# A graph layer on one core: when gathered groups are summed, when fetched destinations are turned, and which engine takes one copy

## The chip, the cores and the metric

The kernel runs on one core of a Trainium2 chip. The metric is device time in microseconds (us), the median of several runs; a separate profiled execution gives the trace. The engines are TensorE (PE in the profile, its weight loads PEld), VectorE (DVE), ScalarE (ACT), GpSimd (POOL) and SyncE (SP). Each engine works through its own instructions strictly in the order in which they were written, and waits on semaphores for the others; DMA transfers are issued from SP, and gathers from POOL. PSUM is the accumulator memory that TensorE writes.

## The reference

One message-passing layer with a residual, on 6250 nodes with 64 features and 206250 edges, sorted by their destination:

```python
h = jnp.maximum(_layernorm(x, axis=-1), 0.0)
msg = h[src] + edge_attr_64
agg = jax.ops.segment_sum(msg, dst, num_segments=6250)
out = x + (jax.nn.relu(agg @ W1 + b1) @ W2 + b2)
```

## The kernel before

The sum over source nodes is made as a product of `h` with a matrix of counts: how often node s is a source of node d. Destinations are cut into windows of 3 nodes ("tiles" of edges), 6 tiles make a *step*, 14 steps a *block* of 84 tiles and 252 nodes; there are 23 blocks (numbers 0 to 22). The program is written as one loop over steps n, with block b = n // 14 and s = n % 14 the step in its block, and what stands at a step goes out on all engines at once:

* every third step VectorE makes one-hot codes for 18 tiles (`hotb`, L975; its inputs `at`, `of` come from `encode`, L958 and L964);
* at every odd step TensorE counts 12 tiles into PSUM (`count`, `pc`, L991; two such buffers), and ScalarE copies them as floats into `ring` (L1004);
* at s = 1, 5 and 7 TensorE multiplies 16, 16 and 17 slices of `h` with the block before (`products`, `pv`, L1013), and at s = 8 VectorE adds the result into the sums (L1045, L1047);
* the edge features are loaded in chunks (`feat`, L491), and at s = 9, 11, 13 summed by destination with a one-hot `hotf` (L504) into a PSUM bank (`chunk_sum`, L515). At s = 0 of the next block `take_sums` (L523) copies the bank to `by_node`, and at s = 3 `chunk_place` (L545) puts it into `pv`. For block 0 the copy is at step 19 and the placing at step 20.

To know where a chunk's edges go, their destinations are needed. They come in five *lots* t = 0 to 4: POOL gathers a lot (`fetch_dst`, the tile `dstq`, 1.5 KB in each of 128 rows), VectorE turns it into numbers within the chunk (`chunk_nodes`, L455 and L456, which wait for the gather's landing), TensorE transposes it (`chunk_turn`, `pdst`, L463), and ScalarE stores it as `rel` (L464). `hotf` of a later block, and some checks at s = 8, read `rel`. The transposes write a PSUM tile with the tag `po`, of which there is one buffer. The same buffer serves, in turn, the two products of the output layer (`mlp_hidden`, `ph`, L1090, read by ScalarE's relu L1092; `mlp_product`, `po`, L1100, read by VectorE L1117) and the value turns of the source lists (`pw`, L796, read by ScalarE L817). Whoever writes it next waits until the last reader is done. The output layer for finished nodes runs at s = 11 (`ph`), 13 (`po`) and 14, from block 9 on.

The last 20 of 202 edge groups (1024 edges each; 182 to 201) take another way: POOL gathers the rows of `h` (`hrows`, L361), VectorE adds them to the edge features (`add_rows`, L1180, at a step that a planner sets from its own estimates of when they have landed), then makes a one-hot (`group_hot`, L566), and two steps later TensorE sums the group (`sum_group`, L576, 8 products), ScalarE copies the result (L578), and three steps after that VectorE adds it into the sums at an address that it reads at run time (`add_sums`, L558). Once a group is summed, its buffer `pfeat` (two of them) is loaded again (L1133), and after `add_rows` the gathers of the next group but one are queued on POOL. At which s a group may be made hot stands in `GROUPS` (1 and 3; in the last block 1 and 5), at most one at each, if a group with its rows added is there. POOL's gathers go out in runs of three, each released by a tiny copy (L1164) that waits for VectorE or for `by_node`.

## Time and profile before

| | us |
|---|---|
| median of 3 runs (377.62, 378.62, 378.67) | 378.62 |
| the profiled execution | 378.36 |
| its span, first to last instruction | 376.7 |
| TensorE busy in it | 333.4 |
| ScalarE, VectorE, POOL busy | 319.4, 318.2, 243.7 |

The span leaves 1.7 us of the profiled execution's time outside. "Busy" of a matmul is modelled, so an engine shown as 100% busy in a stretch is one that was not seen to wait. In the rows of the timeline the columns are: start in us from the span's start, duration in us, engine, line and operation, output and inputs, how many instructions were merged into the row, and in brackets how long the engine sat idle before it and what ended that idle time.

### The profile page before, as it was taken

The page shows a single profiled execution, that of the slowest core. Times are in us where ns is not written, and L with a number is a line of the kernel's source. Part 1 is how long each engine was busy: PE and PEld are TensorE (multiplying, and loading weights), DVE is VectorE, ACT ScalarE, POOL GpSimd, SP SyncE. Part 2 cuts the span into 40 slices and gives each one's busy share as a digit, 9 for nine tenths or more (in the row PEclk, how much of TensorE's full clock was granted, in tenths as well). Part 3 has the DMA queues.
Part 4 walks back from the last instruction along what each step waited for, and adds up shares of the span by engine and source line. Part 5 has one row for each costly group of instructions (what it writes and reads, how often), then busy time and mean ns, then how long its engine had stood idle before and what let it go on. Part 6 is the DMA issues. An engine that isn't in the chain of part 4 may idle for free.

```text
span 376.7 us, 17450 instructions
## 1 busy us (share of the span) xinstructions
PE 333.4 (89%) x7311; PEld 304.7 (81%) x7312; DVE 318.2 (84%) x863; ACT 319.4 (85%) x365; POOL 243.7 (65%) x300
## 2 busy tenths in 40 slices
PE   2055888999989998979999999999999999999993
PEld 1035777988978988968989899989989989998882
DVE  5879998999988999978897998979997898988510
ACT  6678988999789799977999899998999889998820
POOL 8475058888888677675777588887887677721000
PEclk9999999999999999998999999999999999999997
DMA  7855979586685797693876976956967966974400
GB/s 160 269 183 149 339 238 325 153 249 194 199 251 164 211 274 203 172 294 90 264 216 181 288 203 190 293 166 205 303 178 202 307 182 169 278 220 144 124 6 18
DMA packets 97237, 77.75 MB, mean 206 GB/s; under 512 B 14279, under 2 KB 90175, under 8 KB 97152
## 3 DMA queue, kind: packets, MB, share of 16 engines
q1 hardware_dynamic: 88370, 66.72, 58.2%
q0 software_dynamic: 6544, 9.06, 9.9%
q8 instruction: 59, 0.97, 1.1%
q10 hardware_dynamic: 2238, 0.79, 0.9%
q14 instruction: 26, 0.21, 0.2%
HBM read 72.28 MB, written 4.26 MB: 203 GB/s over the span
## 4 chain that ended last, share of the span: by engine, by line
PE 65%; DVE 9%; DMA 7%; ACT 4%; issue 3%; SPq 2%; POOL 1%; DVEq 0%; ACTq 0%; POOLq 0%
PE pv L1013 29%; PE pc L991 11%; PE bank L515 10%; PE ph L1090 4%; PE po L1100 4%; DVE hotb L975 3%; ACT ring L1004 3%; PE bank L576 2%; PE pv L545 2%; DMA feat<-in_edge 2%; DMA dstq<-in_dst_g,cols_i 2%; DMA pfeat<-in_edge 1%; PE pk L789 1%; DVE hotf L504 1%; DMA hrows<-table,src_p 1%
## 5 line engine op out<-in xcount | busy, mean ns | idle before, releaser
L1004 ACT ACTIVATE ring<-pc 128x1764 fp32r<-128x1764 uint8 (+2 forms) x180 | 257.5, 1485 | 24.9 <-PE pc L991 21.0
L361 POOL DMA_INDIRECT hrows<-table,src_p x156 | 170.2, 1091 | 43.9 <-issue 40.6
L1013 PE MATMUL pv<-ring,h 128*128 128x252 f32 (+1 forms) x1127 | 148.6, 285 | 0.4
L1013 PEld LDWEIGHTS pv<-ring,h 128*128 128x128 f32 x1127 | 136.4, 190 | 1.4 <-ACT ring L1004 0.5
L975 DVE TENSOR_TENSOR hotb<-at,of 127x576 int32<-127x576 bf16 x212 | 118.3, 601 | 1.3 <-issue 0.3
L991 PE MATMUL pc<-hotb 128*128 128x49 fp8e5 x1904 | 77.4, 186 | 7.0 <-ACT ring L1004 3.5
L991 PEld LDWEIGHTS <-hotb 128*128 128x128 fp8e5 x1904 | 66.0, 98 | 20.2 <-issue 10.3
L515 PE MATMUL bank<-feat,hotf 128*18 128x64 f32 x3240 | 59.2, 220 | 4.9 <-DVE hotf L504 3.5
L515 PEld LDWEIGHTS bank<-feat,hotf 128*18 128x18 f32 x3240 | 47.1, 98 | 8.5 <-DVE hotf L504 4.3
L504 DVE TENSOR_TENSOR hotf<-rel,iota 128x432 f32<-128x432 bf16 (+1 forms) x68 | 40.7, 600 | 0.1
L1164 POOL COPY root<-root 1x1 f32<-1x1 f32 x43 | 17.3, 403 | 34.7 <-DVE root L1174 34.5
L361 POOL DMA_INDIRECT sums<-in_dst_g,sums x15 | 14.6, 970 | 15.7 <-ACT sums L379 12.0
L958 DVE TENSOR_TENSOR at<-iota_a,kq 128x576 bf16<-128x576 bf16 (+1 forms) x53 | 23.9, 450 | 0.3
L361 POOL DMA_INDIRECT words<-packed,first_i x15 | 17.5, 1167 | 8.4 <-DVE firstp L709 4.2
L1047 DVE TENSOR_TENSOR sums<-sums,pv 128x144 f32<-128x144 f32 (+3 forms) x24 | 7.1, 323 | 18.6 <-PE pv L1013 18.4
L809 ACT ACTIVATE kq<-pk 128x512 bf16<-128x512 f32 (+17 forms) x48 | 17.7, 454 | 3.6 <-PE pk L789 3.6
L964 DVE TENSOR_TENSOR of<-of,kv 128x288 bf16<-128x288 bf16 (+1 forms) x53 | 16.7, 316 | 2.8 <-DVE of L958 0.5
L1092 ACT ACTIVATE after<-ph,b1s 128x504 f32<-128x504 f32 (+4 forms) x16 | 9.4, 589 | 8.1 <-PE ph L1090 8.1
L958 DVE TENSOR_TENSOR of<-iota_w,kq 128x288 bf16<-128x288 bf16 (+1 forms) x53 | 16.0, 301 | 0.0
L523 DVE COPY after<-bank 128x384 f32<-128x384 f32 (+2 forms) x23 | 12.5, 545 | 3.4 <-PE bank L515 3.0
L576 PE MATMUL bank<-after,pfeat 128*64 128x42 f32 x312 | 13.6, 233 | 1.9 <-DVE after L566 1.9
L1090 PE MATMUL ph<-sums,w1s 128*128 128x504 f32 (+4 forms) x32 | 14.7, 542 | 0.4 <-DVE sums L1047 0.4
(203 smaller groups left out, 337.6 us busy)
## 6 DMA issues: line engine op xcount, KB each, us to landing
feat<-in_edge SPq DMA_DIRECT2D x135, 384.0 KB
pfeat<-in_edge SPq DMA_DIRECT2D x19, 256.0 KB
hrows<-table,src_p POOLq DMA_INDIRECT x156
out_y<-after SPq DMA_DIRECT2D x9, 126.0 KB
xl<-in_x SPq DMA_DIRECT2D x2, 512.0 KB
table<-xl SPq DMA_DIRECT2D x2, 512.0 KB
after<-in_x SPq DMA_DIRECT2D x4, 252.0 KB
table<-xl SPq DMA_DIRECT2D x1, 544.0 KB
```

What stands on the lines that cost most here:

```text
L361: nc.gpsimd.indirect_dma_start(out=rows, out_offset=None, in_=source, in_offset=bass.IndirectOffsetOnAxis(ap=index, axis=0), compute_op=op)
L504: nc.vector.tensor_tensor(hot_of[u][:, :n].rearrange("p c j w -> p (c j) w"), rel[:, c:c + n].rearrange("p c q k -> p (c q k)").unsqueeze( ...
L515: nc.tensor.matmul(bank[q * QP:q * QP + WQ, at:at + D], hot_of[u][:, c, j, :], feats[u][c][:, j, :], start=(k == 0), stop=(k == JP - 1))
L576: nc.tensor.matmul(pa[k:k + D, :], tiles[:, j, :], hot[:, j, :], start=(j < 2), stop=(j >= n - 2))
L809: nc.scalar.activation(kq[:, q, at:at + n].rearrange("s i k o -> s (i k) o"), pk[:, q, a:a + n].rearrange("s i k -> s (i k)").unsqueeze(2) ...
L958: nc.vector.tensor_tensor(to[:, :n].rearrange("s i k (m o) -> s (i k) m o", o=2), iota_k.rearrange("s (m o) -> s m o", o=2).unsqueeze(1).t ...
L975: nc.vector.tensor_tensor(hot[:SLOTS, :n, c:c + m * A8].rearrange("s i (w a) -> s i w a", a=A8), at[:SLOTS, o:o + n, k].unsqueeze(2).to_br ...
L991: nc.tensor.matmul(pc[:, at:at + HI], hot[:, :P], hot[:, P:P + HI], start=True, stop=True)
L1004: nc.scalar.activation(to[:, h0:h1], of[:, h0:h1, u:v, :V], AF.Copy)
L1013: nc.tensor.matmul(pvs[b], h2[k][:, h - thirds[k][0], :], ring[:, h, c:c + columns_of_block(b)], start=(h == 0), stop=(h == HI - 1))
L1090: nc.tensor.matmul(ph, w1s, agg[:, a:z], start=True, stop=True)
L1164: nc.gpsimd.tensor_copy(root[0:1], sign)
```

## The change

```diff
-GROUPS = (1, 3)
-LAST_GROUPS = (1, 5)
+GROUPS = {1: 2}
+LATE_GROUPS = {1: 1, 3: 1}
+LAST_GROUPS = {1: 1, 5: 1}
...
     def take_sums(b):
         n = sum(units[u][2] for u in of_block[b]) * D
         by_node[b] = spare["by_node"]
-        nc.vector.tensor_copy(by_node[b][:, :n], bank[:, :n])
+        if b:
+            nc.vector.tensor_copy(by_node[b][:, :n], bank[:, :n])
+        else:
+            nc.scalar.activation(by_node[b][:, :n], bank[:, :n], AF.Copy)
...
     for t in range(1, NT):
         n = 78 + 14 * t
         before.setdefault(n, []).append(lambda t=t: t > 1 and at_once(GATHER_US, lambda: fetch_dst(t)))
-        n = 48 if t == 1 else 87 + 14 * t
+        n = 71 if t == 1 else 93 + 14 * t
         before.setdefault(n, []).append(lambda t=t: chunk_nodes(t))
         before.setdefault(n + 2 + (t > 1), []).append(lambda t=t: chunk_turn(t))
...
-            if s in (GROUPS if b < NW - 1 else LAST_GROUPS) and h_next < added:
+            of = GROUPS if b < NW - 3 else LATE_GROUPS if b < NW - 1 else LAST_GROUPS
+            for _ in range(min(added - h_next, of.get(s, 0))):
                 group_hot(h_next)
                 at_step(n + 2, features_h, h_next)
                 h_next += 1
```

Up to block 19 groups are made hot only at s = 1, up to two of them, and so summed at s = 3 and added at s = 6; before, also one at s = 3, summed at 5 and added at 8. Blocks 20 to 22 stay as they were. The groups that move: 183 waits from block 4 (s = 3) for block 5 and goes with 184; 185 goes from block 6 to block 7, with 186; 188 from block 9 (hot at step 129, summed at 131) to block 10 (141, 143); 189, 190 and 191 each go from s = 3 of blocks 10, 11, 12 to s = 1 of blocks 11, 12, 13; 192 and 193 are summed together in block 14, 194 and 195 in block 16. The others, and from 196 on all, keep their steps. The steps of `add_rows` and POOL's whole order stay. Since a buffer is loaded again when its group is summed, those loads move with the groups.

Lot 1 of the destinations is worked on at step 71 (before 48) and turned at 73 (before 50), both in block 5. Lots 2, 3 and 4 go from steps 115, 129, 143 to 121, 135, 149, and their turns from 118, 132, 146 to 124, 138, 152: from s = 3 and 6 to s = 9 and 12. The gathers that fetch them keep their steps (106, 120, 134). Lot 0 is as before. The copy of block 0's bank goes from VectorE to ScalarE.

Three places in the order that the program writes out. The line numbers in these rows are those of each kernel: the changed one's are higher by 1 up to `chunk_sum` and by 4 below `take_sums` (its L979 is L975 before, its L1008 is L1004, its L464 and L465 are L463 and L464).

The first is VectorE from step 128 to step 131, in block 9. `dstq` is lot 3, the L1180 and L566 are group 188's. Before:

```order
L964 TENSOR_TENSOR of<-of,kv 128x288
L455 TENSOR_SCALAR dstq<-dstq,cols 128x384
L456 SCALAR_TENSOR_TENSOR dstq<-iota_q,cols,dstq 128x384
L975 TENSOR_TENSOR hotb<-at,of 127x18x32
L975 TENSOR_TENSOR hotb<-at,of 127x18x16
L504 TENSOR_TENSOR hotf<-rel,iota 128x432
L1180 TENSOR_TENSOR pfeat<-pfeat,hrows 128x512
L566 TENSOR_TENSOR after<-dst_p,iota 128x336
L755 TENSOR_SCALAR near<-words,nfirst 128x128 x2
```

and with the change:

```order
L968 TENSOR_TENSOR of<-of,kv 128x288
L979 TENSOR_TENSOR hotb<-at,of 127x18x32
L979 TENSOR_TENSOR hotb<-at,of 127x18x16
L505 TENSOR_TENSOR hotf<-rel,iota 128x432
L1184 TENSOR_TENSOR pfeat<-pfeat,hrows 128x512
L759 TENSOR_SCALAR near<-words,nfirst 128x128 x2
```

The two `dstq` instructions and the group's one-hot have left; the addition of the gathered rows has stayed.

The second is TensorE at steps 137 and 138, in the same block, where the first output layer meets the turn of lot 3. Before:

```order
L991 LDWEIGHTS hotb
L991 MATMUL pc<-hotb 128x49
L515 MATMUL bank<-feat,hotf 18x64 x24
L1090 MATMUL ph<-sums,w1s 128x504
L991 LDWEIGHTS hotb
```

and with the change:

```order
L995 LDWEIGHTS hotb
L995 MATMUL pc<-hotb 128x49
L516 MATMUL bank<-feat,hotf 18x64 x24
L1094 MATMUL ph<-sums,w1s 128x504
L464 MATMUL pdst<-shift,dstq 128x128 x3
L995 LDWEIGHTS hotb
```

The three transposes now stand between the layer's first product and the next count; it is the same at steps 151 and 152 with lot 4. Before, they stood six steps earlier, behind `pv` and a group's sum.

The third is ScalarE in block 5, steps 71 to 75, with the turn of lot 1. Before:

```order
L1004 ACTIVATE ring<-pc 128x49x36
L817 ACTIVATE kv<-pw 128x248
L817 ACTIVATE kv<-pw 128x264
L1004 ACTIVATE ring<-pc 128x49x36
L578 ACTIVATE after<-bank 128x42
```

and with the change:

```order
L1008 ACTIVATE ring<-pc 128x49x36
L821 ACTIVATE kv<-pw 128x248
L821 ACTIVATE kv<-pw 128x264
L465 ACTIVATE rel<-pdst 128x384
L1008 ACTIVATE ring<-pc 128x49x36
L582 ACTIVATE after<-bank 128x42 x2
```

The store of `rel` stands behind the two copies of the value turn, whose PSUM buffer the transposes take over, and two groups' results are copied instead of one. On TensorE the transposes stand right behind `pw` there.

## The prediction

> **What bounds the kernel now.** I read the chain of waits first, then the engines' busy time in stretches of 10 us, then the timeline wherever TensorE shows idle time.

> ```profile
> PE 333.4 (89%) x7311; PEld 304.7 (81%) x7312; DVE 318.2 (84%) x863; ACT 319.4 (85%) x365; POOL 243.7 (65%) x300
> PE 65%; DVE 9%; DMA 7%; ACT 4%; issue 3%; SPq 2%; POOL 1%; DVEq 0%; ACTq 0%; POOLq 0%
> 100.00:110.00 10.00, 8.38 (x290) 7.86 (x287) 9.37 (x29) 7.63 (x9) 8.46 (x10) 1.00 0.85 249
> 160.00:170.00 10.00, 7.28 (x149) 6.52 (x146) 7.94 (x22) 7.43 (x6) 7.05 (x9) 1.00 0.92 279
> 170.00:180.00 10.00, 10.00 (x236) 8.86 (x231) 8.35 (x26) 7.74 (x10) 5.69 (x7) 0.83 0.44 121
> 190.00:200.00 10.00, 10.00 (x265) 8.88 (x262) 9.21 (x24) 9.65 (x12) 7.33 (x9) 1.00 0.85 246
> ```

> In the stretches the columns are PE, PEld, DVE, ACT, POOL, granted clock, DMA share, GB/s. TensorE carries the chain. From 170 us on it is seen to wait almost nowhere, so there only its own work and new waits count. Before that it idles in a few places, most of all in 160 to 170, behind which the clock falls to 0.83.

> **What the change removes: the wait in block 9.** The next rows are POOL's gather of lot 3, VectorE, and TensorE.

> ```profile
> 159.46 0.95 POOL L361 DMA_INDIRECT dstq<-in_dst_g,cols_i  x1 [0.30 <-DVE of L958]
> 165.84 2.12 PE L1013 MATMUL pv<-ring,h 128*128 128x252 f32 x16
> 166.04 0.42 DVE L455 TENSOR_SCALAR dstq<-dstq,cols 128x384 f32<-128x384 int32 x1 [1.92 <-DMA dstq<-in_dst_g,cols_i]
> 166.49 0.62 DVE L456 SCALAR_TENSOR_TENSOR dstq<-iota_q,cols,dstq 128x384 f32<-128x384 int16 x1
> 168.58 0.69 DVE L1180 TENSOR_TENSOR pfeat<-pfeat,hrows 128x512 f32<-128x512 f32 x1
> 169.18 0.51 DVE L566 TENSOR_TENSOR after<-dst_p,iota 128x336 f32<-128x336 f32 x1
> 169.74 0.67 PE L576 MATMUL bank<-after,pfeat 128*64 128x42 f32 x16 [1.79 <-DVE after L566]
> 174.70 0.47 PE L991 MATMUL pc<-hotb 128*128 128x49 fp8e5 x12
> 172.00:173.00 1.00, 1.00 (x6) 1.00 (x6) 1.00 (x2) 1.00 (x1) 0.52 (x2) 0.50 0.54 203
> ```

> The lot lands 6.6 us after its issue; VectorE stands still for 1.92 us, everything behind is late, and group 188's one-hot, made two steps before its sum, comes 1.79 us after TensorE wants it. About 1.1 us later the clock is halved for some 3 us (0.17 of 10 us missing, at half rate: 3.4). With the change both `dstq` instructions move behind the next six steps, and the group's one-hot and sum into block 10. `hotb` then starts at about 164.1, and nothing on TensorE waits for L1180. What this gives: `pv` ends at 165.84 + 2.12 = 167.96, and the count after the next `pv` starts at 174.70, 6.74 us on. The same pieces where nothing waits:

> ```profile
> 186.44 0.67 PE L576 MATMUL bank<-after,pfeat 128*64 128x42 f32 x16
> 187.04 0.61 PE L463 MATMUL pdst<-shift,dstq 128*128 128x128 f32 x3
> 187.49 0.46 PE L991 MATMUL pc<-hotb 128*128 128x49 fp8e5 x12
> 189.85 0.47 PE L991 MATMUL pc<-hotb 128*128 128x49 fp8e5 x12
> ```

> Count and `pv` take 189.85 - 187.49 = 2.36. Of the rest, 4.38, a group's sum (187.04 - 186.44 = 0.60) and the transposes (187.49 - 187.04 = 0.45) are only moved: **3.33 us gained**, 1.79 of it the wait and most of the other 1.5 the half clock. The bounds: 1.9 if the clock falls all the same, 3.33 if not. I take 3.33, since the half clock directly follows the longest wait of the second half.

> **What it adds: three waits for the one `po` buffer.** At step 138 the transposes of lot 3 follow `ph` and must wait until ScalarE's relu has read it; at 152 lot 4 does the same.

> ```profile
> 177.09 1.11 PE L1090 MATMUL ph<-sums,w1s 128*128 128x504 f32 x2
> 178.04 0.46 PE L991 MATMUL pc<-hotb 128*128 128x49 fp8e5 x12
> 175.20 3.17 ACT L1004 ACTIVATE ring<-pc 128x1764 fp32r<-128x1764 uint8 x2 [1.33 <-PE pc L991]
> 178.26 0.68 ACT L1092 ACTIVATE after<-ph,b1s 128x504 f32<-128x504 f32 x1
> 193.20 0.46 PE L991 MATMUL pc<-hotb 128*128 128x49 fp8e5 x12
> 193.42 0.69 ACT L1092 ACTIVATE after<-ph,b1s 128x504 f32<-128x504 f32 x1
> ```

> The relu ends at 178.94; with 0.06 for the semaphore (178.26 against the product's end at 178.20) the transposes start at 179.00, where the count started at 178.04: **0.96 lost**, and by 193.42 + 0.69 + 0.06 - 193.20 **0.97** in block 10. Queued behind the wait are the count, whose ring copy ScalarE waits for, and all later TensorE work, which is the bound here, so nothing absorbs it. Below this it cannot go, as the relu must run; upwards each grows by up to a ring copy (3.17 / 2 = 1.59) if ScalarE is behind. I take the lower end, as ScalarE has lost `rel`'s copy from the steps before. `mlp_product` two steps later finds `rel` stored (0.49, row below) before it.

> In block 5 the transposes of lot 1 follow `pw` and wait for ScalarE's two `kv` copies.

> ```profile
> 105.50 0.28 PE L991 MATMUL pc<-hotb 128*128 128x49 fp8e5 x3
> 106.05 1.22 ACT L809 ACTIVATE kq<-pk 128x248 bf16<-128x248 f32 x4
> 107.40 0.40 PE L991 MATMUL pc<-hotb 128*128 128x49 fp8e5 x9 [1.62 <-issue]
> 107.83 1.65 ACT L1004 ACTIVATE ring<-pc 128x1764 fp32r<-128x1764 uint8 x1 [0.56 <-PE pc L991]
> 109.76 0.50 PE L991 MATMUL pc<-hotb 128*128 128x49 fp8e5 x12
> 110.00 0.66 ACT L817 ACTIVATE kv<-pw 128x248 bf16<-128x248 f32 x2 [0.52 <-PE pw L796]
> 164.79 0.32 PE L991 MATMUL pc<-hotb 128*128 128x49 fp8e5 x6 [0.80 <-DVE of L964]
> 0.00:105.90 105.90, 75.58 (x1622) 67.84 (x1623) 95.23 (x253) 88.66 (x113) 70.97 (x106) 1.00 0.76 225
> 0.00:164.30 164.30, 130.41 (x2896) 118.78 (x2897) 149.27 (x412) 141.96 (x173) 115.75 (x155) 1.00 0.76 222
> q8 instruction: 59, 0.97, 1.1%
> ```

> As it stands the wait is 110.66 + 0.06 - 109.76 = 0.96. But just ahead TensorE idles 1.62 us in the middle of a count, with no releaser. It does so once more at 164, and 5793 - 3245 = 2548 multiplications and loads lie between: close to ten times 256, and 59 packets of instructions for 14623 of them are 248 each. I read it as waiting for instructions, at a fixed place in the stream. By then the changed TensorE has issued 38 fewer (group 183's sum 32, the transposes 6), so the place moves behind into `pv` (18 of the count, 20 of the 32 in `pv`, about 1.7 us of work), while its fetch starts only about 0.5 us later: 1.62 shrinks to about 0.4. Then ScalarE sets the pace: kq ends 107.27, ring copy 108.92, `kv` 109.58 or a little more with `pw` late; transposes at 109.7, count at 110.2, against 109.76 + 0.45 moved work. **Block 5: 0**, bounds -0.6 and +0.96; I take 0.

> [...]

> **What costs nothing.** The copy on ScalarE and the two one-hots together:

> ```profile
> 52.75 1.65 ACT L1004 ACTIVATE ring<-pc 128x1764 fp32r<-128x1764 uint8 x1 [0.51 <-PE pc L991]
> 54.58 0.55 PE L545 MATMUL pv<-select,after 128*64 128x42 f32 x12
> 62.48 0.67 PE L515 MATMUL bank<-feat,hotf 128*18 128x64 f32 x24 [0.63 <-DMA feat<-in_edge]
> 187.69 0.49 ACT L464 ACTIVATE rel<-pdst 128x384 bf16<-128x384 f32 x1 [0.33 <-PE pdst L463]
> L566 DVE TENSOR_TENSOR after<-dst_p,iota 128x336 f32<-128x336 f32 (+1 forms) x20 | 9.9, 493 | 0.0
> ```

> ScalarE gets to the copy behind the ring copy, at 54.40, and needs some 0.49 for its 384 columns, so TensorE's placing waits 0.4. Eight us later it waits 0.63 for edge features, whose loads were issued before: covered, else +0.4. POOL's first gathers leave 0.7 later; the first `add_rows` they feed has behind it 2 us of VectorE time, as lot 1 has left. In block 5 VectorE takes 1.04 (lot 1) and 0.49 more ahead of a `hotb` that TensorE needs some 3 us later: free. Lot 2, behind step 120's sums, delays one `hotb` by **0.1**; bound 1.04. TensorE's and ScalarE's numbers of instructions are the same but for that copy, and a moved sum still costs 0.60.

> Sum: -3.33 + 0.96 + 0.97 + 0 + 0.1 = **-1.3 us**. Against the execution's own 378.36 that is 377.1, against the median of the runs, 0.26 higher, 377.3; I say **377.2**.

> **The rivals.**
> * *A, the new waits fall into slack* (375.3): TensorE's 100% hides time in which VectorE or ScalarE set the pace, and the 1.93 us of blocks 9 and 10 cost nothing. For it: ScalarE is at 9.65 of 10 in 190 to 200. Against: the ring copies there wait for TensorE (1.33 above).
> * *B, the half clock stays* (378.6): the stage at 171 comes from something other than the wait, and 1.45 less is gained. For it: the idle of 1.62 at 105.8 drew no such stage. Against: it begins a us behind 1.79 of idle that follows 0.80.
> * *C, slower* (380.4): ScalarE comes to the relu a ring copy late, as the counts reach it closer together; each of the two waits then holds 1.59 more. It decides once ScalarE's copy of the previous count ends after `ph`; at 178.2 both end within 0.2 us of each other. Against: ScalarE has 0.49 less to do just before.
> * *D, block 5 pays* (378.2): the idle at 105.8 stays, or moves on to another place, and the `kv` wait counts in full, +0.96.

> [...]

> **How the numbers follow.** Forecast 0.45 (376.4 to 378.0), A 0.14, B 0.15, C 0.12, D 0.14. A difference under 0.3%, 1.1 us, can't be told from none. Faster: 0.30 of the forecast, A, and 0.04 of B and D, 0.48. Same: 0.15 of the forecast, 0.20 of B and D, 0.35. Slower: C and 0.05 of B and D, 0.17. The range takes in A, and B and D with 0.7 above, and leaves out C: 375.2 to 379.3.

> **What would show it.** Right: L455 no longer waits for a DMA; no idle at L576 in block 9, and a clock of 1.00 in 165 to 180; before the transposes of lots 3 and 4 an idle of 0.9 to 1.0 released by L1092; the 1.62 before L1013's products in block 5 down to under 0.7. Wrong: a clock stage of 0.5 somewhere after all, waits for L1092 of over 2 us, or TensorE waiting for a `hotb` in blocks 5 to 8 for longer than before.

## The result, and the profile after

| | us |
|---|---|
| before, median of 6 executions (377.62 to 381.13) | 378.64 |
| the change, median of 6 (381.06 to 385.61) | 383.73 |
| ratio, with its 95% interval | 1.0128 (1.0087 to 1.0169) |
| the change's profiled execution, and its span | 381.06, 379.3 |

The change made the kernel slower by 1.3%, where 0.4% faster was forecast. The profiled execution is the fastest of the six: its mean granted clock is 0.995, that of the others 0.980 to 0.993, so the trace shows less than the median lost.

The view of TensorE's waits, by what it waited for (total us, times, longest). First the change, then, in a fence of its own, the kernel before:

```profile
PE bank L580 <- ACT after L582: 5.1, 4, 2.0
PE pdst L464 <- ACT after L1096: 1.6, 2, 0.8
PE pdst L464 <- ACT kv L821: 0.8, 1, 0.8
PE pc L995 <- DVE hotb L979: 0.6, 2, 0.4
PE pxn L895 <- issue: 0.6, 1, 0.6
PE bank L516 <- issue: 0.5, 1, 0.5
PE pv L1017 <- issue: 0.2, 1, 0.2
```

```profile
PE bank L576 <- DVE after L566: 1.9, 2, 1.8
PE pc L991 <- issue: 1.6, 1, 1.6
PE pc L991 <- DVE hotb L975: 0.9, 1, 0.9
PE pc L991 <- DVE of L964: 0.8, 1, 0.8
```

The second and third rows of the change are the waits for the `po` buffer that the prediction named. The first is one that it did not: four times TensorE waited 1 to 2 us before a group's sum, for ScalarE's copy (L582) of another group. With the half clock, these rows add up to nearly the difference of the two profiled executions, 381.06 - 378.36 = 2.70: new are 5.1 + 1.6 + 0.8; gone are 1.8 for the one-hot of group 188, 0.3 at the one-hots `hotb`, 1.1 at the pauses that no data ends (1.6 + 0.8 before, the 0.8 listed as L964 among them; 0.6 + 0.5 + 0.2 now), and 1.7 for the half clock (a stage of 3.4 us at half rate, which the trace before has and the trace of the change has not). That makes 7.5 - 4.9 = 2.6; the changes in the rows not shown cancel.

The wait in the timeline of the change, at the pair of block 7 (two sums at one step):

```profile
137.98 0.92 DVE L570 TENSOR_TENSOR after<-dst_p,iota 128x336 f32<-128x336 f32 x2
138.53 0.67 PE L580 MATMUL bank<-after,pfeat 128*64 128x42 f32 x16
138.75 0.75 ACT L821 ACTIVATE kv<-pw 128x408 bf16<-128x408 f32 x2
139.28 1.76 ACT L1008 ACTIVATE ring<-pc 128x1764 fp32r<-128x1764 uint8 x1
140.80 0.34 ACT L582 ACTIVATE after<-bank 128x42 f32<-128x42 f32 x1
141.19 0.67 PE L580 MATMUL bank<-after,pfeat 128*64 128x42 f32 x16 [1.98 <-ACT after L582]
```

The first group's sum ends at 139.20. Its copy stands on ScalarE behind the `kv` copies and a ring copy, runs from 140.80 to 141.14, and only then does the second sum start. The two groups use different columns of one PSUM tile, `bank` (`b = g % 2` in `sum_group`), and both one-hots were ready: what orders them is that the program writes sum, copy, sum, copy, and the second sum, a write to the tile, starts 0.05 us behind the end of the copy, the last read of it. Before, two groups were never summed at one step, and the copy was long done. The other pairs, in blocks 5, 14 and 16, waited 0.96, 0.99 and 1.18.

### The profile page after: what moved, and what is told of

The parts are those of the page before. It is cut to its first block, busy times and chain, and to the rows that moved or that the text cites. A ratio compares the mean times of both kernels' runs of the same rounds, so it can differ in the third digit from the quotient of the medians.

```text
span 379.3 us, 17435 instructions
## 1 busy us (share of the span) xinstructions
PE 332.4 (88%) x7311; PEld 303.2 (80%) x7312; DVE 317.4 (84%) x862; ACT 319.8 (84%) x366; POOL 245.5 (65%) x300
## 4 chain that ended last, share of the span: by engine, by line
PE 48%; ACT 5%; DVE 2%; issue 2%; POOL 2%; DMA 1%; DVEq 0%; ACTq 0%; POOLq 0%
PE pv L1017 21%; PE bank L516 8%; PE pc L995 8%; PE po L1104 4%; ACT ring L1008 3%; PE ph L1094 3%; PE bank L580 2%; PE pv L549 2%; DMA hrows<-table,src_p 1%; PE pk L793 1%; POOL hrows L362 1%; ACT kq L813 1%; DVE hotb L979 1%; POOL words L362 1%; ACT after L1096 1%
## 5 line engine op out<-in xcount | busy, mean ns | idle before, releaser
L1008 ACT ACTIVATE ring<-pc 128x1764 fp32r<-128x1764 uint8 (+2 forms) x180 | 258.1, 1484 | 26.4 <-PE pc L995 23.2
L979 DVE TENSOR_TENSOR hotb<-at,of 127x576 int32<-127x576 bf16 x212 | 118.2, 601 | 1.0
L995 PEld LDWEIGHTS <-hotb 128*128 128x128 fp8e5 x1904 | 65.2, 98 | 15.9 <-issue 7.5
L516 PE MATMUL bank<-feat,hotf 128*18 128x64 f32 x3240 | 60.2, 220 | 5.5 <-DVE hotf L505 3.2
L580 PEld LDWEIGHTS bank<-after,pfeat 128*64 128x64 f32 x312 | 11.7, 138 | 5.9 <-ACT after L582 5.6
L1096 ACT ACTIVATE after<-ph,b1s 128x504 f32<-128x504 f32 (+4 forms) x16 | 9.4, 589 | 8.1 <-PE ph L1094 8.1
L1168 POOL COPY root<-after 1x1 f32<-1x1 f32 x22 | 7.7, 352 | 12.8 <-DVE after L525 9.6
```

The costliest lines, as they stand in the source:

```text
L516: nc.tensor.matmul(bank[q * QP:q * QP + WQ, at:at + D], hot_of[u][:, c, j, :], feats[u][c][:, j, :], start=(k == 0), stop=(k == JP - 1))
L580: nc.tensor.matmul(pa[k:k + D, :], tiles[:, j, :], hot[:, j, :], start=(j < 2), stop=(j >= n - 2))
L979: nc.vector.tensor_tensor(hot[:SLOTS, :n, c:c + m * A8].rearrange("s i (w a) -> s i w a", a=A8), at[:SLOTS, o:o + n, k].unsqueeze(2).to_br ...
L995: nc.tensor.matmul(pc[:, at:at + HI], hot[:, :P], hot[:, P:P + HI], start=True, stop=True)
L1008: nc.scalar.activation(to[:, h0:h1], of[:, h0:h1, u:v, :V], AF.Copy)
L1168: nc.gpsimd.tensor_copy(root[0:1], sign)
```

## The experiments

**Both sums, then both copies.** The order on every engine stays that of the change, instruction for instruction; only what the second sum waits for differs.

```diff
+    def features_of(gs):
+        copies = []
+        for g in gs:
+            read_bases(g, 1)
+            copies.append(sum_group(g, parts_of.pop(g), copied=False))
+        for g, copy in zip(gs, copies):
+            copy()
+            if g + ROWS < G:
+                load_h(g + ROWS)
...
-                at_step(n + 2, features_h, h_next)
+                at_step(n + 2, features_of, gs)
```

> The change with one thing reordered: where two groups are summed at one step, both sums are written before ScalarE's two copies, so that the second sum no longer has to wait for the copy of the first out of the shared PSUM tile. Every engine has the same instructions in the same order as in the change. Theory P (the pair's wait is what the change lost): the four waits of 0.96, 1.98, 0.99 and 1.18 us before a second sum are gone, the profiled execution comes to about 376 (381.06 less 5.1), the median to 376 to 378.5, and the mean granted clock is no lower than before's. Rival R (the new waits for the po buffer and the later one-hots set the time): the median stays at 382 or more. Rival K (the clock falls in the changed kernel for another cause than those waits): the waits go, but the median stays 2 us or more above the profiled execution, at 379 to 381, with mean clocks of about 0.98.

Measured: 376.01 (375.18 to 377.96), ratio to the kernel before 0.9941 (0.9913 to 0.9969). The pair of block 7 in its timeline:

```profile
139.03 1.13 PE L580 MATMUL bank<-after,pfeat 128*64 128x42 f32 x32
139.26 0.75 ACT L825 ACTIVATE kv<-pw 128x408 bf16<-128x408 f32 x2
139.79 1.76 ACT L1012 ACTIVATE ring<-pc 128x1764 fp32r<-128x1764 uint8 x1
140.10 0.47 PE L999 MATMUL pc<-hotb 128*128 128x49 fp8e5 x12
141.31 0.44 ACT L583 ACTIVATE after<-bank 128x42 f32<-128x42 f32 x2
```

The 32 products run in 1.13, the copies are as late as before, and nobody waits for them. The change as it stands is 7.7 us slower than this kernel (383.73 - 376.01, beside 378.64 and 378.85 for the kernel before). 5.1 of it are the waits; the other 2.6 go along with the clock, of which the median over the executions is 0.994 here and 0.9845 in the change, but that the waits lower the clock is argued, not shown, by this run. Theory P holds in the median, and R falls. P's number for the profiled execution, about 376, was missed: it is 377.96, the slowest of the eight, with a half-clock stage at 63 us. K falls for the most part: the clock comes back with the waits gone.

**The groups at their old steps**, with the rest of the change:

```diff
-GROUPS = {1: 2}
+GROUPS = {1: 1, 3: 1}
```

> The change with the groups at their old steps (one at s = 1, one at s = 3); the later destinations and the copy on ScalarE stay. Theory P: no pair is left, and the sum of the prediction holds for the rest: 376.4 to 378.0, with 0.8 us of wait each before the transposes of lots 3 and 4. Rival R: 381 or more, since the waits for the po buffer are all still there.

Measured: 379.23 (377.19 to 382.19), ratio 1.0009 (0.9978 to 1.0040). No pair, no loss; but the 1.3 us of the prediction's sum aren't there either. TensorE's waits in its trace:

```profile
PE pc L995 <- issue: 1.5, 1, 1.5
PE pc L995 <- DVE hotb L979: 1.4, 3, 0.9
PE pdst L464 <- ACT after L1096: 0.8, 1, 0.8
PE pdst L464 <- DVE root L1178: 0.8, 1, 0.8
PE pdst L464 <- ACT kv L821: 0.7, 1, 0.7
```

The wait of 1.8 in block 9 is gone, but the pause of 1.5 in block 5 has stayed, and the three waits of the transposes stand beside it. That is as the prediction's rival D has it; but here group 183's sum, whose move was to shorten the pause, stays where it was, so the run is no full test of D.

**The groups alone** at their new steps; destinations and copy as before, sum and copy of a pair in turn.

> Of the change only the groups' new steps; destinations and the copy as before. Theory P: four waits before a second sum, 5 us in all, against some 1.8 to 3.3 us gained in block 9, since group 188 no longer stands behind the late lot: 380 to 383. Rival R: 378.6 or less, as no transposes stand behind the relu.

Measured: 383.89 (380.31 to 385.33), ratio 1.0124 (1.0078 to 1.0170): the whole loss of the change, without the destinations, and 0.9 more than theory P's 383. Four waits for ScalarE's copy, 5.6 us. Here the half clock also follows a wait before a second sum, of 2.00 us, from 140.39 to 142.39; busy time and granted clock in stretches of 1 us (columns as above):

```profile
140.00:141.00 1.00, 0.39 (x14) 0.27 (x10) 1.00 (x5) 1.00 (x4) 0.69 (x2) 1.00 0.95 281
141.00:142.00 1.00, 0.00 (x0) 0.00 (x0) 1.00 (x3) 1.00 (x1) 0.83 (x1) 1.00 1.10 345
142.00:143.00 1.00, 0.61 (x12) 0.61 (x14) 1.00 (x5) 0.34 (x2) 0.86 (x1) 0.65 1.01 331
143.00:144.00 1.00, 1.00 (x23) 0.92 (x20) 0.90 (x4) 0.21 (x1) 0.81 (x3) 0.50 0.98 323
144.00:145.00 1.00, 1.00 (x8) 1.00 (x6) 0.90 (x4) 0.87 (x1) 0.69 (x2) 0.50 0.79 171
145.00:146.00 1.00, 1.00 (x8) 1.00 (x8) 1.00 (x3) 0.78 (x1) 0.70 (x1) 0.65 0.64 238
```

**The turns ahead of the layer's first product**, pairs as in the change:

```diff
-        n = 71 if t == 1 else 93 + 14 * t
+        n = 71 if t == 1 else 92 + 14 * t
...
-        before.setdefault(n + 2 + (t > 1), []).append(lambda t=t: chunk_turn(t))
+        before.setdefault(n + 2, []).append(lambda t=t: chunk_turn(t))
```

> The change with lots 2 to 4 worked on one step sooner (s = 8) and turned two steps sooner (s = 10), ahead of the layer's first product instead of behind it; the pairs stay. Theory P: the two waits of 0.8 us for the relu go, 1.6 us in all, and the pairs' 5.1 us stay: profiled execution about 379.5, median 381 to 383. Rival R: 378 or less, as the waits for the relu are gone.

Measured: 382.92 (381.91 to 385.92), ratio 1.0133 (1.0096 to 1.0171). The two waits for the relu are gone from the trace, 0.6 for lot 3's own numbers has come, and the time isn't told apart from the change's. The waits for the relu were not what made it slow. P's median holds; its number for the profiled execution, about 379.5, was missed (382.85).

**Pairs alone, without the wait**, destinations and copy as before:

> The kernel of the pairs alone, both sums ahead of the copies, once more: its first run fell on a chip on which the kernel before took 474 us with TensorE pausing all over the program, so nothing could be told there. Theory P (the waits are all that the pairs cost): 5 us under the same kernel with the copies between (383.9), so 377 to 379. Theory L (the later destinations carry the gain of the kernel with everything, 376.0): no less than 378, with VectorE still waiting about 1.9 us for lot 3 in block 9 and TensorE about 1.5 for the one-hots behind it. Rival G (pairing carries the gain, since group 188 leaves block 9 and TensorE's pause without a releaser in block 5 gets shorter): 376 to 377.

Measured: 374.79 (371.94 to 379.82), ratio 0.9906 (0.9867 to 0.9944). Against the groups alone with sum and copy in turn (1.0124) the order of two calls in the program is worth 2.2%, with the same instructions on every engine. Its timeline in block 9, where the prediction wanted the destinations out of the way:

```profile
162.29 0.42 DVE L456 TENSOR_SCALAR dstq<-dstq,cols 128x384 f32<-128x384 int32 x1 [0.40 <-DMA dstq<-in_dst_g,cols_i]
164.84 0.68 DVE L1185 TENSOR_TENSOR pfeat<-pfeat,hrows 128x512 f32<-128x512 f32 x1
165.09 2.22 PE L1018 MATMUL pv<-ring,h 128*128 128x252 f32 x17
168.68 0.31 PE L996 MATMUL pc<-hotb 128*128 128x49 fp8e5 x6 [1.21 <-DVE hotb L980]
```

Lot 3 is still worked on there, and VectorE waits 0.40 for it. With group 188 gone from the block, TensorE goes on to the next `pv` and waits 1.21 for a one-hot, where it waited 1.79. This is a lucky trace, the fastest of the twelve executions: the lot landed 5.0 us after its issue, and 6.6 in the kernel before. In the trace of the groups alone, with the lots at the same steps, it landed 6.3 us after its issue, and the waits are larger:

```profile
170.68 0.47 DVE L456 TENSOR_SCALAR dstq<-dstq,cols 128x384 f32<-128x384 int32 x1 [1.62 <-DMA dstq<-in_dst_g,cols_i]
177.12 0.31 PE L992 MATMUL pc<-hotb 128*128 128x49 fp8e5 x6 [1.53 <-DVE hotb L976]
```

G holds for the median, and goes further than it said; but the groups' move alone does not take the wait behind the late lot away, as theory L had it for this block.

**The change without the wait, and one part taken back at a time**: the turns of lots 2 to 4 ahead of the product, as in the diff above; then lot 1 at steps 48 and 50 (`48 if t == 1`); then block 0's copy on VectorE.

> The change with both sums of a pair ahead of their copies and the turns of lots 2 to 4 ahead of the layer's first product, once more. If the waits of 0.8 us for the relu lie on the path: 376.0 less 1.6, plus up to 0.65 for VectorE's work on lot 3: 374.4 to 375.3. If they fall into slack: 376.0.

Measured: 378.11 (375.21 to 380.81), ratio 0.9999 (0.9960 to 1.0038).

> The change with both sums of a pair ahead of their copies and lot 1 back at steps 48 and 50, once more. If the wait of 0.75 us for the kv copies in block 5 lies on the path: 375.3; if VectorE's 1.04 us in block 3 is paid for: 376 to 377.

Measured: 374.25 (373.51 to 375.79), ratio 0.9913 (0.9876 to 0.9949).

> The change with both sums of a pair ahead of their copies and block 0's copy back on VectorE, once more. If the copy costs and gains nothing: 376.0 within 0.5; if ScalarE's lateness in block 1 is paid for: 375.7; if VectorE's relief there is worth its 0.5 us: 376.5.

Measured: 377.38 (374.49 to 378.96), ratio 0.9967 (0.9929 to 1.0005).

The first came out slower than both of its expectations. Its two waits for the relu are gone, but its executions spread over 5.6 us, and its profiled one, 380.77, has 2.4 us of pauses that no data ends ahead of 66 us and three half-clock stages (its mean clock is 0.981); of TensorE's waits there:

```profile
PE bank L516 <- issue: 2.5, 3, 1.7
PE pc L999 <- DVE hotb L983: 1.3, 1, 1.3
PE pdst L464 <- ACT kv L825: 0.7, 1, 0.7
PE pxn L899 <- issue: 0.7, 1, 0.7
```

So this run doesn't settle what the turns' place is worth. Between the marks of blocks 10 and 11 in the table below it gains 0.31 on the kernel before where the kernels with late turns lose 1.2; there the wait is on the path. Lot 1's move looks like the part whose return gives most: 374.25, below both of its expectations, is 1.8 below the first kernel of this section and 3.1 below the one with the copy on VectorE, which both have lot 1 late. As ratios, 0.9913 against 0.9941 and 0.9967, the intervals overlap. In the table below, the stretch from block 3 to 5 is 2.1 us shorter with lot 1 early than in the first kernel: 0.45 are the transposes, which then stand ahead of block 3's mark, 0.75 is the wait, and two pauses that no data ends, 0.67 and 0.47, are in the first kernel's trace alone. The kernel with the copy on VectorE came out above all three of its expectations. The copy's own share isn't told apart: 0.9967 with it on VectorE against 0.9941 on ScalarE, and the intervals overlap.

Where in the program each kernel stands against the one before, from the starts of VectorE's addition of `pv` at s = 8 in the profiled executions (minus is ahead, us). "No wait" is the first experiment, "pairs alone" and "lot 1 early" are those without the wait too:

| block | before, start | change | no wait | pairs alone | lot 1 early | turn early |
|---|---|---|---|---|---|---|
| 1 | 57.63 | 0.05 | 0.10 | -0.92 | 0.10 | 0.62 |
| 3 | 85.72 | 0.33 | 1.44 | -0.92 | 1.60 | 4.13 |
| 5 | 115.95 | 1.79 | 2.14 | -2.08 | 0.18 | 5.67 |
| 8 | 158.10 | 1.30 | 1.15 | -2.20 | -0.77 | 6.06 |
| 9 | 174.89 | -1.30 | -1.69 | -4.85 | -3.62 | 3.40 |
| 10 | 190.04 | -1.80 | -2.27 | -6.20 | -4.20 | 2.09 |
| 11 | 204.65 | -0.62 | -1.09 | -6.71 | -3.02 | 1.78 |
| 16 | 275.38 | 2.73 | -0.60 | -6.20 | -2.51 | 2.56 |

The rows behind two of its entries, of the kernel before and of the change:

```profile
158.10 0.47 DVE L1047 TENSOR_TENSOR sums<-sums,pv 128x144 f32<-128x144 f32 x2
174.89 0.42 DVE L1047 TENSOR_TENSOR sums<-sums,pv 128x252 f32<-128x252 f32 x1 [0.31 <-PE pv L1013]
```

```profile
159.40 0.48 DVE L1051 TENSOR_TENSOR sums<-sums,pv 128x144 f32<-128x144 f32 x2
173.59 0.40 DVE L1051 TENSOR_TENSOR sums<-sums,pv 128x252 f32<-128x252 f32 x1
```

Behind block 16 the distances stay within 0.4 us. From block 1 to 3 they move by up to 3.5 us between kernels that differ in nothing that matters there: in these blocks TensorE waits for edge features, in another way each time (1.3 us in the kernel before, 1.5 in the change, 2.3 without the wait and with the copy on VectorE), and half-clock stages fall there, as the one at 63 us in the first experiment.

**Runs in another condition.** Ten runs met a condition of the chip in which the kernel before takes 474 to 489 us, so that they can't be compared with the others. Four are the kernels from "pairs alone" to the copy on VectorE, a first time (e5 to e8):

> Of the change only the groups' new steps, with both sums of a pair written before the two copies; destinations and block 0's copy as before. The pairs' waits are gone here. Theory P (those waits are all that the pairs cost): 5 us under the same kernel with the copies between (383.9), so 377 to 379. Theory L (the later destinations carry the gain of the kernel with everything, 376.0): no less than 378, with VectorE still waiting about 1.9 us for lot 3 in block 9 and TensorE about 1.5 for the one-hots behind it. Rival G (pairing carries the gain, since group 188 leaves block 9 and TensorE's pause without a releaser in block 5 gets shorter): 376 to 377.

> The change with both sums of a pair ahead of their copies, and lots 2 to 4 worked on at s = 8 and turned at s = 10, ahead of the layer's first product. If the waits of 0.8 us for the relu lie on the path: 376.0 less 1.6, plus up to 0.65 for VectorE's work on lot 3, which the transposes then wait for: 374.4 to 375.3. If they fall into slack: 376.0.

> The change with both sums of a pair ahead of their copies, and lot 1 back at steps 48 and 50. If the wait of 0.75 us for the kv copies in block 5 lies on the path: 376.0 less 0.75, so 375.3; VectorE's 1.04 us for the lot, back in block 3, is paid for if TensorE's waits for one-hots there grow: then 376 to 377.

> The change with both sums of a pair ahead of their copies, and block 0's copy back on VectorE. The prediction's reading is that the copy costs and gains nothing: 376.0 within 0.5. If ScalarE's lateness in block 1 is paid for (the placing waits 0.25 us for it): 375.7; if VectorE's relief there is worth its 0.5 us: 376.5.

Measured, as ratios to the kernel before there: 0.9984 (0.9926 to 1.0042), 1.0148 (1.0083 to 1.0213), 1.0110 (1.0047 to 1.0172) and 1.0229 (1.0169 to 1.0289). In this condition three of the four are slower than the kernel before, so what the other runs say of them is not shown for every chip.

The others were to settle what moving lots 2 to 4 gives: lot 1 early and the turns ahead of the product (e13), the same with the copy on VectorE (e14), and all destinations at their old steps (e16), each without the wait of the pairs; then repetitions of the first and the last.

> Both sums of a pair ahead of their copies, lot 1 at its old steps, lots 2 to 4 worked on at s = 8 and turned at s = 10, ahead of the layer's first product; the copy of block 0 on ScalarE. If the move gains in block 9 and gives it back behind the relu (0.8 us in block 9, 0.8 in block 10), this kernel keeps it: 1.0 to 1.6 under the same with turns behind the product (374.25, 0.9913 of before), so 372.7 to 373.3, or 0.987 of before. If the move has nothing to gain once the group has left block 9: 374.3, 0.991.

> The kernel before this one in the list (both sums first, lot 1 at its old steps, lots 2 to 4 turned at s = 10) with block 0's copy back on VectorE. If the copy's engine costs and gains nothing: the same within 0.5 us. If the 1.4 us by which the other pair of kernels differed (377.38 against 376.01, on two chips) belongs to the copy: 1.4 slower.

> Both sums of a pair ahead of their copies, block 0's copy on ScalarE, and every lot of destinations at its old steps. If moving lots 2 to 4 gains by itself: slower than 374.25 (0.9913 of before) by 1 us or more, with VectorE waiting 1.9 us for lot 3 and TensorE 1.2 for the one-hots behind it. If the groups' move carried the gain of block 9: 374.3 or less, 0.991 or less.

Measured: 1.0023 (0.9941 to 1.0105), 0.9993 (0.9933 to 1.0053) and 1.0078 (1.0009 to 1.0147).

> Once more: both sums of a pair ahead of their copies, lot 1 at its old steps, lots 2 to 4 worked on at s = 8 and turned at s = 10, ahead of the layer's first product; the copy of block 0 on ScalarE. If the move gains in block 9 and gives it back behind the relu (0.8 us in block 9, 0.8 in block 10), this kernel keeps it: 1.0 to 1.6 under the same with turns behind the product (374.25, 0.9913 of before), so 372.7 to 373.3, or 0.987 of before. If the move has nothing to gain once the group has left block 9: 374.3, 0.991.

> Both sums of a pair ahead of their copies, lot 1 at its old steps, lots 2 to 4 worked on at s = 8 and turned at s = 10, ahead of the layer's first product; the copy of block 0 on ScalarE. If the move gains in block 9 and gives it back behind the relu (0.8 us in block 9, 0.8 in block 10), this kernel keeps it: 372.7 to 373.3, or 0.987 of before. If the move has nothing to gain once the group has left block 9: 374.3, 0.991.

> Both sums of a pair ahead of their copies, block 0's copy on ScalarE, and every lot of destinations at its old steps. If moving lots 2 to 4 gains by itself: slower than 374.25 (0.9913 of before) by 1 us or more. If the groups' move carried the gain of block 9: 374.3 or less, 0.991 or less.

Measured: 1.0060 (0.9983 to 1.0137), 1.0037 (0.9989 to 1.0085) and 1.0065 (0.9979 to 1.0151). Whether a kernel with lot 1 early, the turns ahead of the product and no wait beats 374.3 stays open.

## Why the prediction was wrong, step by step

* **The step that failed** is in "What costs nothing": TensorE's number of instructions is the same, "and a moved sum still costs 0.60". The second sum of a pair costs 0.60 and a wait for ScalarE's copy, 0.96, 1.98, 0.99 and 1.18 us: 5.1, against a sum of -1.3. With both sums ahead of the copies the same kernel gains, so these waits are what turned the forecast gain into a loss. The prediction followed the three waits for one PSUM buffer, `po`, and did not ask the same of the other buffer that the change makes two writers meet in, `bank`. In all four pairs the second sum waited for the copy, though it writes other columns; whether only the order that the program sets for any two users of one tile holds it back, no run here shows. With sums before copies the rest of the change comes to 0.9941, 2.2 us under the kernel before where 1.3 was forecast.
* **Block 9, -3.33**: from block 8's mark to block 10's the kernel before takes 31.94, the change 28.84. Of those 3.10 us, 0.60 (one group's sum) has only moved on behind block 10's mark, and 0.80 of new wait is in it: 3.10 - 0.60 + 0.80 = 3.3 removed; 3.6 without the pairs' waits. (The transposes cancel: lot 4's have left the stretch, and lot 2's have come in, as the rows below show.) The size was right. How much of it each move gives is less clear: with the lots moved and the group left, the same reckoning gives 3.1, and the 1.8 of wait is gone; with the group moved and the lots left, it gives 3.4 in the lucky trace of the pairs alone and 2.1 in that of the groups alone, and 1.2 to 1.5 of wait stays. So the two moves overlap for the most part: credited one by one they would count more than 3.6, and the lots' move pays 1.6 behind the relu. In the medians it shows no gain on top of the groups' (0.9913 with it, lot 1 early and the copy on ScalarE; 0.9906 without).
* **The waits behind the relu, 0.96 and 0.97**: 0.80 each, as the prediction's mechanism has it.
* **Block 5, 0**: `kv` is waited for 0.76, and the pause has moved into `pv`, behind its 11th product, and shrunk from 1.62 to 0.20, much as written (20 of its 32 instructions would be the 10th, and 0.4 was named). From block 3's mark to block 5's the change takes 1.46 more, 0.96 of it the pair and 0.45 lot 1's transposes, which stood just ahead of block 3's mark before: about 0 for the rest, as written. What this 0 hides is that the groups' move alone makes the stretch 1.2 us shorter in its trace (pairs alone in the table: -0.92 to -2.08), a gain that the kernels with lot 1 late do not show.
* **The copy on ScalarE**: the placing waits 0.3 for it, 0.4 was named; its price can't be told from nothing.
* **The rivals.** B, the half clock stays, is wrong of the place: the profiled execution has no such stage between 165 and 180. It may be right of the kernel: the other five executions have clocks of 0.980 to 0.993, so that stages are likely in them, but no trace shows where. C gave the right sign, which was luck: its 380.4 is about a third of the loss, and its mechanism isn't there, as no wait for L1096 is longer than 0.8. The signs named for being right were nearly all seen (the line that was L455 no longer waits for a DMA, no idle before a group's sum in block 9, full clock from 165 to 180, 1.62 down to 0.20; the idle behind the relu was 0.80 instead of 0.9 to 1.0), and the kernel was slower all the same: none of the rivals, and nothing in "what would show it", covered a wait of one group for another; the chance of 0.17 on slower was held by C for the most part.

Lot 2's transposes before, at 154.71, ahead of block 8's mark:

```profile
154.71 0.51 PE L463 MATMUL pdst<-shift,dstq 128*128 128x128 f32 x3
```

The prediction's smaller steps in the timeline of the change, at lot 1's turn, at lot 2's transposes, now behind block 8's mark, and at the turns of lots 3 and 4:

```profile
105.94 1.53 PE L1017 MATMUL pv<-ring,h 128*128 128x252 f32 x11
107.67 0.84 PE L1017 MATMUL pv<-ring,h 128*128 128x252 f32 x5 [0.20 <-issue]
109.51 0.61 PE L464 MATMUL pdst<-shift,dstq 128*128 128x128 f32 x3 [0.76 <-ACT kv L821]
112.33 0.67 PE L580 MATMUL bank<-after,pfeat 128*64 128x42 f32 x16 [0.96 <-ACT after L582]
...
161.60 0.61 PE L464 MATMUL pdst<-shift,dstq 128*128 128x128 f32 x3
...
175.63 0.69 ACT L1096 ACTIVATE after<-ph,b1s 128x504 f32<-128x504 f32 x1
176.37 0.61 PE L464 MATMUL pdst<-shift,dstq 128*128 128x128 f32 x3 [0.80 <-ACT after L1096]
...
192.35 0.61 PE L464 MATMUL pdst<-shift,dstq 128*128 128x128 f32 x3 [0.80 <-ACT after L1096]
```

## What to carry to other kernels

When a change puts two pieces of work side by side that stood apart, list every buffer that both touch, with its readers, before counting instructions: here two sums in different columns of one PSUM tile were tied together by the copy that the program writes between them. Where two such pieces have their data ready together, write both writers first and the readers behind them: here the order on the engines stayed the same, and 7.7 us came back. And where two edits aim at the same wait, credit it once, and try each alone.

## What the runs showed of the hardware

**Pauses without a releaser.** In the same traces, from 50 us on, the profile shows 27 pauses of TensorE, of 0.17 to 1.66 us, that no data ended, and 26 of these stand 192 to 197 instructions past a multiple of 256 in its stream (multiplications, loads and separate waits counted). The place is fixed, the length is not: at one of them 0.20, 0.47, 0.49, 0.64, 0.74, 1.03, 1.55 and 1.62 us, and nothing in two kernels. The prediction read the pause as waiting for instructions; what TensorE waits for there, no trace shows.

**A chip in another condition.** In the first run of the change without the wait and with the turns early (473.6 us of span), VectorE's and ScalarE's instructions take what they take in the kernel before (the one-hot `hotf`, 128x432, 0.60 us in both, a full ring copy mostly 1.6 to 1.7 in both), but TensorE pauses 112 times with no releaser, ahead of products of seven lines. Those with the largest sums among its waits:

```profile
PE bank L516 <- issue: 31.3, 71, 1.1
PE pc L999 <- issue: 13.3, 31, 0.8
PE pk L797 <- issue: 3.2, 2, 3.0
```

The mean granted clock there is 0.92. One chip was in this condition and 23 minutes later was not. A gain of 1% that the other runs show isn't seen there; three of the kernels are 1.1 to 2.3% slower than the kernel before.
